# Seven block products for each projection of a pair of heads, in a decoder layer whose first stage is a delta rule

## The chip, the cores and the metric

The kernel runs on one core of a Trainium2 chip. The metric is the device time of one execution in microseconds (us). Before the change the median of three runs is 3437.4 us (3436.95 to 3442.61). A core has five engines that run beside one another, each with a queue of its own: PE multiplies matrices, DVE (VectorE), ACT (ScalarE) and POOL (GpSimd) work on vectors, and SP (SyncE) issues most of the transfers. SBUF is the working memory on the chip, PSUM the memory into which PE writes.

## What is computed

One decoder layer on x of 4 batches x 512 tokens x 512 channels, all in f32: a gated delta rule, then cross-attention with rounded (fake-quantised) values, then self-attention and a mixture of experts. The change touches the first of them alone. Its reference, cut:

```python
q = _causal_conv(x @ Wq.T, cw_q, cb_q)     # conv over 4 tokens per channel, then silu
k = _causal_conv(x @ Wk.T, cw_k, cb_k)
v = _causal_conv(x @ Wv.T, cw_v, cb_v)
...
def step(Sstate, inputs):                  # 16 heads of 128 channels, 512 steps
    retrieved = einsum('bhkv,bhk->bhv', Sstate, k_t)
    error = v_t - g_t[..., None] * retrieved
    Snew = g_t[..., None, None] * Sstate + k_t[..., :, None] * (beta_t[..., None] * error)[..., None, :]
    o_t = einsum('bhkv,bhk->bhv', Snew, q_t)
...
o = o * rsqrt(mean(o * o) + EPS) * norm_w
o = o * silu(x @ Wg.T)
return o @ Wo.T
```

Each of the four weights Wq, Wk, Wv and Wg is 2048 x 512, so that one head's projection of one batch is a product of 128 x 512 by 512 x 512.

## The kernel before

The first stage works through 32 **pairs of heads** (`NP = B * NHG`: 4 batches x 8 pairs of 2 heads). Three stages of work belong to a pair m. `stage1` (L597) makes k and q: projection, conv, transposes, the triangular matrix `at` with its decays, and the products of q with k. `stage2_inverse` (L723) inverts the blocks of `at` in 31 small steps of two operations on POOL (on DVE for pairs 0 and 1), with a way through DRAM at its start and end. `stage2_values` (L768) makes v and the gate g. `stage3` (L813) runs through the four chunks of 128 tokens with a state that each chunk hands to the next, and `output` (L933) multiplies with Wo.

A projection is made in `conv` (L572). For each head it runs four matmuls with 512 columns into one PSUM bank (L578), one for each block of 128 input channels. For q, k and v follow an Identity with scale and bias on ACT (L586), three shifted multiply-adds on DVE that read the projection in PSUM (L589), and a Silu on ACT (L592); for g a Silu alone (L582). The weights of a pair and one projection come in one load of 512 KB (`load_weights`, L564), one buffer for each of the four projections.

**What sets the order.** DVE, ACT and POOL issue their instructions in the order in which the program writes them (`manual_schedule`, L1050). The program is a set of Python generators that yield between steps, and `turns` (L192) takes steps of each in rotation. In the loop of L1066, iteration m takes a step of `stage3(m)` and then one turn of the rest: two steps of `stage1(m + 2)`, one of `stage2_values(m + 1)`, two of the inversions, one of the next batch's `prologue`, where there is one, and one of `output(m - 1)`. `stage3` has some 15 steps; what is left of the others afterwards runs behind it.

Other lines that the steps below name: L642 the scan that makes the decays of a head (one instruction over 4 chunks, with the table `id4`), L666 to L668 `product` (q with k), L685 the multiply of q with its decay on POOL, L698 to L704 the squares of q summed over channels, L731 and L732 the inversion's two operations, L881 `r` and L903 the state in `stage3` on DVE, L888 the matmul that needs `r`, L911 and L928 larger POOL operations of `stage3`, L957 the sums of `output`, L972 the sum with x at a batch's end. `x_kT` and `wpj` (L1074 to L1083) are operands of cross-attention, loaded in the last two iterations, in which the cross-attention of the first tokens already begins.

Of the kernel before, what the change touches and what calls it, by code (L numbers as in the profile page):

```python
# [31 lines left out]
F32 = mybir.dt.float32  # L32
BF16 = mybir.dt.bfloat16
# [29 lines left out]
C_UP, C_LO, C_ONE, C_ID4, C_INV, N_TAB_A = 0, 1, 2, 3, 7, 7 + 8 // GRP  # L63
# [3 lines left out]
def _tables():  # L67
# [10 lines left out]
    ta[:, C_ID4 : C_ID4 + 4] = (r == c)[:, None, :]  # L78
# [26 lines left out]
def decoder(ctx: ExitStack, tc: tile.TileContext, a: dict, out: bass.AP):  # L105
# [21 lines left out]
    def rsqrt(dst, src, pool, add=0.0, mul=1.0):  # L127

        n = src.shape[1]
        t = pool.tile([P, 64], F32, name="rsq")  # L130
        nc.vector.tensor_scalar(t[:, :n], src, mul, add, ALU.mult, ALU.add)  # L131
        nc.gpsimd.tensor_tensor(dst, t[:, :n], mhalf[:, :n], ALU.pow)  # L132
# [233 lines left out]
    with ExitStack() as st:  # L366
# [16 lines left out]
        id4 = tab_a[:, C_ID4 : C_ID4 + 4, :].rearrange("p a b -> p (a b)")  # L383
# [21 lines left out]
        r_d = [dram.tile([HG * TB, P], F32, name=f"r_d{n}") for n in range(SLOTS)]  # L405

# [42 lines left out]
        def prologue(b):  # L449
# [18 lines left out]
            for c in range(TB):  # L468
# [7 lines left out]
                if c == 0:  # L476
                    xnT = s2.tile([P, KD, S], F32, name="xnT", bufs=2)
                    seqs[b] = [xnT]
# [18 lines left out]
            g_a, lg, beta, gam, ngam, gend, gall = (seq.tile([P, H1, TB], F32, name=n) for n in ("g_a", "lg", "beta", "gam", "ngam", "gend", "gall"))  # L497
# [60 lines left out]
            yield  # L558

        sums = {}  # L560

        weights = {}

        def load_weights(m, *what, by=nc.sync):  # L564

            for n in what:
                if m < B * NHG:
                    t = (s1 if n < 2 else s2).tile([P, KD, HG * P], F32, name=f"w{n}", bufs=1)
                    by.dma_start(t, a["a_w"][m % NHG][:, n])
                    weights[m, n] = t  # L570
# [24 lines left out]
        keys, pairs = {}, {}  # L595

        def stage1(m):  # L597
# [3 lines left out]
            wk, wq = weights.pop((m, 1)), weights.pop((m, 0))  # L601

            def rows(n):
                t = s1.tile([P, HG, S], F32, name=f"row{n}", bufs=1)
# [3 lines left out]
            kT, kt = [], []  # L608
            ss = small.tile([P, HG * TB], F32, name="ss", bufs=2)
            for p in range(HG):  # L610
                t = live.tile([P, S], F32, name="kT")
                yield from conv(b, hg, p, 1, wk, t)
                kT.append(t)
                yield
            xnT, beta, gam, ngam, gend, gall = seqs[b]
            gb = rows(0)
            load_weights(m + 1, 1)
# [21 lines left out]
            for p in range(HG):  # L639

                e = s1.tile([P, TB, P], F32, name="em")
                nc.vector.tensor_tensor_scan(chunks(e), gb[p], id4, 0.0, ALU.mult, ALU.add)  # L642
# [17 lines left out]
            qh, qg, pt, sq, kd_ = [], [], [], [], []  # L660

            def product(p):
# [4 lines left out]
                t = live.tile([P, TB, P], F32, name="pt", bufs=6)  # L667
                nc.vector.tensor_tensor(t, pq, em[p], ALU.mult)  # L668
                pt.append(t)

# [5 lines left out]
            for p in range(HG):  # L676
                q = s1.tile([P, S], F32, name="qh")
                c = conv(b, hg, p, 0, wq, q)
                yield from itertools.islice(c, 2)
                if p:  # L680
                    product(0)
                yield from c
                qh.append(q)
                g = live.tile([P, S], F32, name="qg", bufs=6)
                nc.gpsimd.tensor_tensor(g, q, mb[p], ALU.mult)  # L685
                qg.append(g)
                t = w2.tile([P, S], F32, name="cv", bufs=5)
                nc.scalar.activation(t, q, AF.Square)
                sq.append(t)
                yield  # L690
            load_weights(m + 1, 0)
            decayed(0)
            yield
# [11 lines left out]
            yield  # L705
            product(1)
# [3 lines left out]
            keys[m] = (kT, kd_, qg, pt, nr, rq)  # L710
# [57 lines left out]
        def stage2_values(m):  # L768
# [3 lines left out]
            wv, wg = weights.pop((m, 2)), weights.pop((m, 3))  # L772
            v_, gs = [], []
            for p in range(HG):
                t = yield from conv(b, hg, p, 2, wv, None)
                yield
# [963 lines left out]
```

## Time and profile before

| what | value |
|---|---|
| median of the runs | 3437.4 us (3436.95 to 3442.61) |
| the profiled execution's own time | 3435.95 us |
| its span (first to last instruction) | 3434.2 us |
| granted TensorE clock, mean | 0.978 |
| the projections' matmuls (L578) | 2048 records, 592 ns median length, from 19.8 to 1802.2 us |
| the shifted multiply-adds (L589) | 576, mean 746 ns |
| inversion on POOL (L731, L732) | 930 each, mean 344 and 372 ns |
| DMA over the span | 473.97 MB, mean 138 GB/s |

The profile is one execution on the chip. A busy row gives an engine's busy time and its share of the span. The row of 40 slices gives the busy share in tenths. A group row has the line, engine, operation, output and inputs by name, shape and count, then busy time, the mean length of one instruction and the idle time before them with what ended it. [...] The delta rule lies in about the first 1880 us of the span.

### The profile page before, as it was taken

How to read it: one execution, taken by the hardware profiler on the slowest of the kernel's cores; microseconds unless marked ns; L12 is line 12 of the kernel's file. 1: busy time of each engine (PE TensorE's matmuls, PEld its weight loads, DVE VectorE, ACT ScalarE, POOL GpSimd, SP SyncE). 2: the span in 40 equal slices, each digit the busy share in tenths (PEclk: the TensorE clock that was granted, in tenths of full speed). 3: DMA queues.
4: the chain of work that ended last, by engine and by line, in shares of the span. 5: the costliest groups of instructions: out<-in, count | busy, mean ns of one | idle time of the engine just before them, and what ended most of it. 6: DMA issues, size and time to landing. Idle time of an engine off the chain costs nothing. (4 is left out here: it accounts for less than half of the span.)

```text
span 3434.2 us, 49083 instructions
## 1 busy us (share of the span) xinstructions
PE 3253.7 (95%) x16596; PEld 1815.8 (53%) x16596; DVE 1836.7 (53%) x4155; ACT 1600.1 (47%) x4336; POOL 1449.6 (42%) x2766
## 2 busy tenths in 40 slices
PE   5899999999999999999997899999999999999996
PEld 2455555555555555555554455555555545554443
DVE  5755565555645556555545566656655665655111
ACT  3445555455554555455534345455454545534121
POOL 1156766667566675766752211121112111212442
PEclk7999999999999999999998899999999999999998
DMA  6343434534445343453432654445445544546444
GB/s 172 111 124 110 135 110 123 162 110 130 112 122 157 117 134 110 123 151 114 131 103 68 226 181 158 144 159 186 152 142 164 167 153 145 159 165 221 90 83 95
DMA packets 462250, 473.97 MB, mean 138 GB/s; under 512 B 199199, under 2 KB 310821, under 8 KB 461808
## 3 DMA queue, kind: packets, MB, share of 16 engines
q1 hardware_dynamic: 448656, 440.66, 42.2%
q0 software_dynamic: 11904, 27.34, 3.9%
q8 instruction: 132, 2.16, 0.3%
q10 hardware_dynamic: 1440, 2.84, 0.3%
q14 instruction: 118, 0.97, 0.1%
HBM read 410.15 MB, written 64.81 MB: 138 GB/s over the span
## 5 line engine op out<-in xcount | busy, mean ns | idle before, releaser
L578 PE MATMUL pb<-xnT,w 128*128 128x512 f32 x2048 | 959.4, 603 | 0.1
L578 PEld LDWEIGHTS pb<-xnT,w 128*128 128x128 f32 x2048 | 364.3, 192 | 337.4 <-issue 330.9
L589 DVE SCALAR_TENSOR_TENSOR cv<-pb,pp,cv 128x510 f32<-128x510 f32 (+2 forms) x576 | 424.3, 746 | 99.0 <-ACT cv L586 85.7
L732 POOL TENSOR_TENSOR iT<-iT,iW 64x126 f32<-64x126 f32 (+22 forms) x930 | 345.6, 372 | 72.8
L1229 PE MATMUL pb<-c_q,hT 128*128 128x512 f32 x768 | 362.9, 611 | 2.9 <-DMA c_q<-in_c_wk_dram 2.7
L731 POOL TENSOR_TENSOR iW<-iA,iT 64x126 f32<-64x126 f32 (+22 forms) x930 | 320.2, 344 | 65.8 <-issue 0.2
L952 PE MATMUL pb<-wot,og 128*128 128x512 f32 x512 | 246.0, 604 | 6.4 <-DVE xa L957 4.3
L1153 POOL TENSOR_TENSOR rope_s<-q,tab 128x128 f32<-128x128 f32 x64 | 36.6, 572 | 461.2 <-DVE q L1259 403.4
L1229 PEld LDWEIGHTS pb<-c_q,hT 128*128 128x128 f32 x768 | 144.6, 197 | 157.2 <-issue 153.5
L586 ACT ACTIVATE cv<-pb,pp 128x512 f32<-128x512 f32 x192 | 148.7, 774 | 147.5 <-PE pb L578 143.6
L633 POOL TENSOR_TENSOR rk<-ss,mhalf 128x8 f32<-128x8 f32 x32 | 78.0, 2438 | 277.3 <-DVE ss L632 277.3
L957 DVE TENSOR_TENSOR xa<-pb,xa 128x512 f32<-128x512 f32 x112 | 77.1, 689 | 189.8 <-PE pb L952 189.7
L1325 PE MATMUL po<-eT,val 128*128 128x512 f32 x320 | 167.2, 619 | 11.6 <-ACT eT L1323 8.6
L295 ACT ACTIVATE x_e<-pb,nm,x_step 128x256 f32<-128x256 f32 x256 | 141.2, 563 | 75.5 <-DVE nm L291 68.0
L1295 PE MATMUL pb<-kT,qT 128*128 128x256 f32 (+3 forms) x576 | 166.5, 416 | 0.7 <-ACT og L1301 0.6
L1335 PE MATMUL pw<-wot,oT 128*128 128x512 f32 x344 | 163.5, 602 | 0.4 <-DVE oT L1327 0.2
L685 POOL TENSOR_TENSOR qg<-qh,row 128x512 f32<-128x512 f32 x64 | 82.1, 1283 | 176.7 <-ACT qh L592 153.9
L952 PEld LDWEIGHTS pb<-wot,og 128*128 128x128 f32 x512 | 92.2, 191 | 101.8 <-issue 88.9
L1630 PE MATMUL pb<-w_gu,eT 128*128 x312 | 142.1, 599 | 2.0 <-issue 2.0
L1323 ACT COPY eT<-pb 128x512 f32<-128x512 f32 x160 | 90.8, 594 | 107.1 <-PE pb L1321 106.8
L592 ACT ACTIVATE qh<-cv 128x512 f32<-128x512 f32 x64 | 40.3, 630 | 213.0 <-DVE cv L589 205.1
L132 POOL TENSOR_TENSOR rms_r<-rsq,mhalf 128x1 f32<-128x1 f32 x48 | 27.4, 571 | 245.1 <-DVE rsq L131 245.0
(390 smaller groups left out, 6216.6 us busy)
## 6 DMA issues: line engine op xcount, KB each, us to landing
c_q<-in_c_wq_dram SPq DMA_DIRECT2D x128, 512.0 KB
w<-in_a_w_dram SPq DMA_DIRECT2D x124, 512.0 KB
wot<-in_c_wo_dram SPq DMA_DIRECT2D x86, 512.0 KB
row<-g_d SPq DMA_DIRECT2D x64, 512.0 KB
c_o<-in_c_wo_dram SPq DMA_DIRECT2D x42, 512.0 KB
at_d<-at SPq DMA_DIRECT2D x64, 256.0 KB
T<-t_d SPq DMA_DIRECT2D x32, 512.0 KB
X<-x_d SPq DMA_DIRECT2D x32, 512.0 KB
```

The costliest lines, as they stand in the source:

```text
L295: nc.scalar.activation(e[:, 2 * r + g, :], ps[r][:, g, :], AF.Exp, bias=nm[:, r, g : g + 1], scale=step[:, h : h + 1], accum_out=ssum[:, g ...
L578: nc.tensor.matmul(pj, wt[:, kd, p * P : (p + 1) * P], xnT[:, kd, :], start=kd == 0, stop=kd == KD - 1)
L586: nc.scalar.activation(ac, pj, AF.Identity, bias=cb[:, m, h : h + 1], scale=cw[:, m, h, 3:4])
L589: nc.vector.scalar_tensor_tensor(ac[:, j:], pj[:, : S - j], cw[:, m, h, 3 - j : 4 - j], ac[:, j:], ALU.mult, ALU.add)
L731: eng.tensor_tensor(u, A[:, i, i + 1 :].unsqueeze(2).to_broadcast([nb, n, w]), T[:, i, :w].unsqueeze(1).to_broadcast([nb, n, w]), ALU.mult)
L732: eng.tensor_tensor(T[:, i + 1 :, :w], T[:, i + 1 :, :w], u, ALU.add)
L952: nc.tensor.matmul(pw, og[p][:, c * P : (c + 1) * P], wot[:, p, :], start=p == 0, stop=p == HG - 1)
L1229: nc.tensor.matmul(pj, hT[:, kd, :], w[:, kd % 2, :], start=kd == 0, stop=kd == KD - 1)
L1295: nc.tensor.matmul(ps[:, m, k * P : (k + w) * P], qT[g][:, n + m, :], kT[:, g, j : j + w, :], start=True, stop=True)
L1325: nc.tensor.matmul(po, val[:, g, :], eT, start=k == 0, stop=k == c)
L1335: nc.tensor.matmul(pw, oT[:, h + m, :], w[:, m, :], start=g == 0 and h + m == 0, stop=g == 3 and h + m == 3)
L1630: nc.tensor.matmul(pg, hT[:, kd, :], w_gu[:, bass.ds(e, 1), kd, :, :], start=kd == 0, stop=kd == KD - 1)
```

## The change

Two heads' projection is one product of weights (512 inputs x 256 outputs) with the input (512 x 512 tokens). The change cuts each into 2 x 2 blocks: inputs in halves of 256, outputs by head, tokens in halves of 256. Strassen's algorithm, in the form with few additions, makes the four result blocks from seven block products in place of eight; each block product is two matmuls of 256 columns. It needs four sums of weight blocks, four of input blocks, and seven sums that put the products together.

- **Weight sums.** In the first batch, the weights are loaded in two transfers per projection, summed in place (four operations of 128 x 256, `combine`, on POOL or DVE), and the seven blocks are kept in DRAM (`seven_d`). Later batches load all seven blocks in one transfer of 896 KB. All projections share three buffers `w`; a fixed list `order` says which is loaded, summed and stored next.
- **Input sums.** `differences` makes four on POOL, once for each batch.
- **Result sums.** `seven` copies two blocks from PSUM on ACT, adds five on DVE with one operand in PSUM, and adds two in SBUF on POOL. The result lies in SBUF, where Identity, the multiply-adds and Silu then read it, first for both heads.
- **What stays.** k and q of pairs 0 and 1, and v and g of pair 0, run as before (`is_plain`).
- **Room.** Both decay rows share a buffer, as do q and its product with the decay; the scan runs in four pieces with `ident` in place of `id4`; `xnT` has one buffer per parity of batch; `pt` has five buffers instead of six, and `product(1)` and `decayed(1)` wait until `stage3` is done (`busy`); `x_kT` is loaded in the last iteration instead of the one before; `wk` of the cross-attention's keys lies in other tiles.

The diff, cut to its core:

```diff
+        order = [(0, 1), (0, 0), (1, 1), (0, 2), (1, 0), (0, 3)]
+        for m in range(B * NHG):
+            order += [(m + 2, 1), (m + 1, 2), (m + 2, 0), (m + 1, 3)]
...
+        def is_plain(m, n):
+            return m < (2 if n < 2 else 1)
...
+        def differences(b, t1):
+            xnT = seqs[b][0]
+            t = (s2 if b % 2 else s1).tile([P, 3, 2, S // 2], F32, name="xd", bufs=1)
+            b11, b12, b21, b22 = (xnT[:, 2 * k : 2 * k + 2, n * S // 2 : (n + 1) * S // 2] for k in range(2) for n in range(2))
+            for dst, x, y in ((t[:, 1], b22, b12), (t1, b12, b11), (t[:, 0], b22, t1), (t[:, 2], b21, t[:, 0])):
+                nc.gpsimd.tensor_tensor(dst, x, y, ALU.subtract)
+                yield
+            moving[b] = (b11, b21, t1, t[:, 2], t[:, 0], t[:, 1], b22)
...
+        def combine(eng):
+            u = order[stages["combine"]] if stages["combine"] < len(order) else None
+            if u in fresh:
+                a11, a12, s1_, a22, s2_, s3_, s4_ = (fresh[u][:, n] for n in range(7))
+                for dst, x, y, op in ((s3_, a11, s1_, ALU.subtract), (s1_, s1_, a22, ALU.add), (s2_, s1_, a11, ALU.subtract), (s4_, a12, s2_, ALU.subtract)):
+                    eng.tensor_tensor(dst, x, y, op)
...
+        def used(m, n):
+            i = order.index((m, n))
+            keep_them()
+            combine(nc.gpsimd if m < 3 else nc.vector)
+            load()
+
+        def seven(b, n, wt, dst):
+            x = moving[b]
+            def products(*ns):
+                ps = p_b.tile([P, 2, S // 2], F32, name="pb")
+                for k, n in enumerate(ns):
+                    for kd in range(2):
+                        nc.tensor.matmul(ps[:, k], wt[:, n, kd, :], x[n][:, kd, :], start=kd == 0, stop=kd == 1)
+                return ps[:, 0], ps[:, 1]
...
+            l, r = products(0, 4)
+            nc.scalar.copy(c11, l)
+            plus(c12, c11, r)
+            yield
+            l, r = products(5, 2)
+            nc.scalar.copy(c22, r)
+            plus(c21, c12, l)
+            plus(c12, c12, c22, nc.gpsimd)
+            plus(c22, c21, c22, nc.gpsimd)
+            yield
+            l, last_ = products(1, 3)
+            plus(c11, c11, l)
+            yield
+            l, _ = products(6)
+            plus(c21, c21, last_)
+            plus(c12, c12, l)
+            yield
...
+            yield from seven(b, n, wt, dst)
+            used(m, n)
+            for p in range(HG):
+                h = hg * HG + p
+                ac = w2.tile([P, S], F32, name="cv", bufs=5)
+                nc.scalar.activation(ac, dst[p], AF.Identity, bias=cb[:, n, h : h + 1], scale=cw[:, n, h, 3:4])
+                for j in range(1, 4):
+                    nc.vector.scalar_tensor_tensor(ac[:, j:], dst[p][:, : S - j], cw[:, n, h, 3 - j : 4 - j], ac[:, j:], ALU.mult, ALU.add)
+                yield
+                res.append(ac)
+            for p in range(HG):
+                nc.scalar.activation(res[p] if n == 2 else dst[p], res[p], AF.Silu)
+            yield
...
-                nc.vector.tensor_tensor_scan(chunks(e), gb[p], id4, 0.0, ALU.mult, ALU.add)
+                for c in range(TB):
+                    nc.vector.tensor_tensor_scan(e[:, c, :], gb[p][:, c * P : (c + 1) * P], ident, 0.0, ALU.mult, ALU.add)
...
+            yield from convs(m, 0, qh)
+            square(0)
+            square(1)
+            yield
+            product(0)
+            yield
             decayed(0)
...
+            while busy:
+                yield
             product(1)
...
+                x_kT = v_keep.tile([P, 3, KD, M], BF16, name="x_kT")
+                nc.sync.dma_start(x_kT, x_kT_d)
...
+            busy.append(m)
             for _ in stage3(m):
                 next(rest, None)
+            busy.clear()
```

## The prediction

> **What bounds the kernel now.** I read the page's busy rows and slices first, then the engines' busy time inside the delta-rule stage, then groups by form, then the order of time on PE, DVE and POOL.
>
> ```profile
> span 3434.2 us, 49083 instructions
> PE 3253.7 (95%) x16596; PEld 1815.8 (53%) x16596; DVE 1836.7 (53%) x4155; ACT 1600.1 (47%) x4336; POOL 1449.6 (42%) x2766
> ...
> PE   5899999999999999999997899999999999999996
> ...
> POOL 1156766667566675766752211121112111212442
> PEclk7999999999999999999998899999999999999998
> ```
>
> PE is full from slice 2 to slice 20, the stage that the change edits; POOL, 42% over the span, is at 60 to 70% there. The table of engine busy time for 200 to 1700 us (columns: stretch, length, PE, PEld, DVE, ACT, POOL, granted clock, DMA share, GB/s):
>
> ```profile
> 200.00:1700.00 1500.00, 1480.97 (x8709) 862.01 (x8709) 822.63 (x1423) 777.27 (x2195) 1002.68 (x2128) 1.00 0.44 127
> ```
>
> 28 pairs of heads pass in it (rows with one instruction per pair count 28), so a pair takes 1500/28 = 53.6 us: PE 52.9, POOL 35.8, DVE 29.4, ACT 27.8. PE's clock is whole. The stage is bound by PE, and the 24 us that DVE idles per pair are mostly waits for PE:
>
> ```profile
> POOL rk L633 <- DVE ss L632: 216.8, 28, 11.9
> DVE xa L957 <- PE pb L952: 170.4, 69, 3.8
> ACT cv L586 <- PE pb L578: 124.6, 62, 2.9
> ```
>
> **PE: what the seven products take away.** The projection group has 2048 records for 4 x 32 x 2 x 4 = 1024 matmuls of the code, so an f32 matmul counts twice. Busy time is no price, since records overlap; the distance from start to start is. In order of time (start, length):
>
> ```profile
> 1001.44 1.88 PE L578 MATMUL pb<-xnT,w 128*128 128x512 f32 x4
> 1003.16 0.61 PE L888 MATMUL ps<-r,X 128*128 128x128 f32 x4
> ```
>
> Four 512-column records from 1001.44 to 1003.16: 0.430 us each. Half the columns with a new weight block each time is seen in attention:
>
> ```profile
> 2995.72 1.03 PE L1295 MATMUL pb<-kT,qT 128*128 128x256 f32 x4
> 2996.58 0.61 PE L311 MATMUL pb<-ident_i,x_ei 128*128 128x128 bf16 x8
> ```
>
> Four in 0.86 us: 0.215 each, exactly half, so the doubled number of weight loads per column costs nothing visible. A projection of a pair was 8 matmuls, 16 x 0.430 = 6.88 us; it becomes 14 matmuls, 28 x 0.215 = 6.02. It saves 0.86. Of 4 x 32 = 128 projections 6 stay plain (k and q of pairs 0 and 1, v and g of pair 0): **122 x 0.86 = 105 us off PE**, 3.44 per pair. PE's floor falls from 53.6 (its present gaps kept) to 50.1 us per pair.
>
> **What comes on the other engines.** Prices from groups by form:
>
> ```profile
> L589 DVE SCALAR_TENSOR_TENSOR cv<-pb,pp,cv 128x510 f32<-128x510 f32 x168 | 125.8, 749 | 5.9
> ...
> L685 POOL TENSOR_TENSOR qg<-qh,row 128x512 f32<-128x512 f32 x56 | 71.4, 1275 | 115.0 <-ACT qh L592 93.7 <-issue 21.4
> ...
> L642 DVE TENSOR_TENSOR_SCAN em<-row,tab_a 128x512 f32<-128x512 f32 x56 | 65.3, 1208 | 0.0
> ```
>
> and, for 128x256 with one operand in PSUM, from the later stages:
>
> ```profile
> L1633 DVE TENSOR_TENSOR xa<-xa,pb 128x256 f32<-128x256 f32 x39 | 16.4, 421 | 184.1 <-ACT xa L1632 184.1
> ```
>
> - DVE: five 128x256 adds with one PSUM operand per projection, 5 x 0.42 x 4 = 8.4 us per pair. The scan in four pieces: nothing if time goes with columns; at most three extra fixed costs of 0.2 (a scalar_tensor_tensor of 128 columns takes 0.34, of 512 0.745, so 0.2 is there without columns), 1.2 per pair for two scans. I take 0.9. DVE: 29.4 + 9.3 = 38.7.
> - ACT: two 128x256 copies per projection at 0.37 (L700, same size from PSUM): 2.9 per pair; 30.7. Silu of g from SBUF is 0.63 against 0.60: nothing.
> - POOL: two 128x256 adds per projection. 64x136 takes 0.47, 128x512 1.275; between them some 0.75. 8 x 0.75 = 6.0; 41.8 per pair. The q multiply is only moved.
> - Weight sums: 32 sets of four 128x256 operations. Eight fall to POOL (8 x 4 x 0.75 = 24 us, in the prologue and the first two iterations, where POOL was 10 to 25% busy until 200 us), 24 to DVE in iterations 1 to 7: 24 x 4 x 0.42 = 40 us, about 6 per pair. There DVE is at 45 of 50. Each waits for its load, issued one projection earlier; behind a late one DVE's or POOL's whole queue waits.
> - Input differences: four 128x512 POOL operations per batch, 5 us, once per batch: in the numbers above, nothing. Bounds 0 to 5 us for the first, which runs ahead of iteration 0.
> - DMA: 6 x 0.5 + 32 x 0.5 MB, 32 stores and 90 loads of 0.92 MB instead of 128 x 0.52: 64 MB more over 1.7 ms, 38 GB/s beside 127 at 44% share. Three buffers, loaded three projections (some 38 us) ahead: cost 0; if that cover went, SP's queue (T, X, rrow loads behind it) would stop on a buffer. Bounds 0 to 10 us.
> - x_kT is loaded one iteration later, with wpj. The wpj load was issued at 1802.8 and the first matmul on x_kT ran at 1804.6. 0.77 MB will not have landed: 3 us lost, bounds 0 to 8.
> - Buffers: both decay rows share one, so the second row's load waits for the scans and holds SP's queue until then; its reader, the POOL multiply, comes some four turns later: 0, bounds 0 to 1 us per pair. The second head's product and its scaling on ACT move behind stage3: PE work of 0.9 us per pair that no longer fills gaps inside stage3 but fills the end of the iteration: 0, bounds -0.5 to 0.9 per pair. The smaller tables and rsq tiles cost nothing, since no instruction goes with them.
>
> **The coupling.** Two things decide how much of 105 us arrives. First, the convolution's three scalar_tensor_tensors read PSUM and SBUF today; after, both tensors lie in SBUF, as do those of L972. What that does beside POOL is in the trace:
>
> ```profile
> 1052.05 0.74 DVE L972 SCALAR_TENSOR_TENSOR xa<-xa,a_rs,x_in 128x512 f32<-128x512 f32 x1
> ...
> 1056.18 1.16 DVE L972 SCALAR_TENSOR_TENSOR xa<-xa,a_rs,x_in 128x512 f32<-128x512 f32 x1
> ```
>
> ```profile
> 1055.52 1.27 POOL L911 TENSOR_TENSOR gs<-gs,rrow 128x512 f32<-128x512 f32 x1
> 1056.75 0.76 POOL L731 TENSOR_TENSOR iW<-iA,iT 64x81 f32<-64x81 f32 x1
> ```
>
> The first L972 runs between POOL's work in 0.74; the second starts inside L911 and takes 1.16, and POOL's next takes 0.76 where its group's mean is 0.37. So each delays the other by about 0.4 when they meet. There will be 18 such DVE operations per pair; if each catches one POOL instruction, POOL gets 18 x 0.39 = 7 us and stands at 48.8, DVE some 18 x 0.2 = 3.6 (between nothing and 0.42) and stands at 42. Both are still under 50.1, POOL just so.
>
> The Trainium skill ("SBUF — State Buffer", Who interferes with whom) says that a VectorE instruction with two SBUF inputs and a GpSimd instruction that reads SBUF exclude each other for the whole instruction. By that rule POOL's 41.8, 18 x 0.745 and two scans of 1.2 could not overlap at all: 57.6 us per pair, an estimate, some 120 us slower in 30 pairs. The rows above agree that they exclude each other, but only in part: the second L972 ended 0.2 us sooner than a start after L911 would allow.
>
> Second, hand-overs. A conv went PE, ACT, DVE, ACT; now it goes PE, ACT, DVE, POOL, DVE, ACT, DVE, ACT, and each wait holds an in-order queue: behind DVE's wait for POOL's sums stand r and state of stage3, for which PE waits. Chain after the last product: 2 x 0.42 + 0.775 + 3 x 0.745 + 0.63 = 4.5 us for the first head, 6.7 for the second, against 3.6 before. Cover in the order of emission: two to three turns of about 3.4 us before a transpose or product uses it. So mostly hidden, with little left when POOL is a turn late. Per pair the loss lies between 0 and 3.4 us (all the gain) or beyond; I take a third of the gain, 1.2, because POOL has 1.3 of 50.1 us free for waits where it has 18 today.
>
> **Sum**, against the profiled execution's own 3435.95 us (span 3434.2 and 1.75 around it): -105 + 31 x 1.2 (37) + first batch, DVE near full, 6 x 2 = 12 + x_kT 3 = -53: 3383. The median of the runs lies 1.45 above that execution: **3385**.
>
> **Rivals.**
> - Nearly all of it arrives (waits under 0.5 us per pair): 3340 to 3360. For it: DVE's idle time is mostly waiting for PE. Chance 0.15.
> - **Slower: POOL becomes the bound.** Place: the inversion's small operations among the convs of two heads. It passes PE when POOL gets 8.3 us of delays per pair, and passes today's 53.6 at 11.8, which is 30 of its 84 instructions held 0.39 us; 18 DVE operations catching two each give 36, 14 us: 55.8 per pair, 2.2 x 30 = 66 and 15 for the first batch and x_kT on top: up to 3515; where POOL's waits add only 1 us per pair to 53.6, 3470. For it: POOL's long wait for ss cannot be filled, since its queue is in order. Against: the count of one catch each. Chance 0.36.
> - Nothing: gain and waits cancel, 3430 to 3444. Chance 0.08.
> - That 256 columns do not run at half: excluded by L1295.
>
> **How the numbers follow.** Forecast case 3360 to 3430: 0.41. Faster 0.41 + 0.15 = 0.56; within 0.2% (7 us, about what a measurement of this kernel can tell from no change) 0.08; slower 0.36. Range 3340 to 3470: it leaves out some 0.05 below and 0.14 above. The forecast case's own range is 3360 to 3430.
>
> **What would show it.** Right: PE's projection records 3416 of 256 columns at 0.215 start to start, pair time 51 to 52 us, POOL 80 to 95% in the stage. POOL's inversion groups 10 to 20% longer than today, conv operations above 0.8. Wrong: PE idle before L888 or its conv consumers with DVE as releaser, and DVE waiting on POOL's sums: then POOL or the chain is the bound. Wrong the other way: PE still 98% busy and the pair at 50.

## The result and the profile after

The kernel after takes 3661.0 us (median of 4 runs, 3659.5 to 3662.7) against 3437.2 of the kernel before on the same chip: ratio 1.0653, 95% interval 1.0631 to 1.0675. It is 224 us slower where 52 us less was forecast, far outside the range. The page of the kernel after, busy rows and slices:

```profile
span 3660.7 us, 53930 instructions
...
PE 3252.2 (89%) x18060; PEld 2139.6 (58%) x18060; DVE 2163.0 (59%) x5053; ACT 1681.6 (46%) x4580; POOL 1851.2 (51%) x3059
...
PE   5778878899889888898888789999999999999997
...
POOL 1368777888778888688888221112111211211442
PEclk7889999999999999999999889999999999999998
```

PE is no longer full in the slices of the delta-rule stage, which now ends in slice 23; no other engine is full in its place. Nearly everything happens inside the delta-rule stage: from the first `og` of pair 0 to that of pair 31 it takes 1889.7 us against 1682.4 (+207), the work ahead of it 14 more, the work behind it 5 more.

Below, an **ordinary pair** is one without a batch's edge or a prologue beside it (the mean of eight, from one pair's first `og` to the next one's): 52.8 us before, 56.4 after. Over 31 pairs these 3.6 us make 112 of the 207 us; the others lie in the first batch and in the four pairs around each later prologue, which take 62 to 69 us in the second batch against 53 to 60 before. The engines' busy time over two ordinary pairs, before and then after (stretch, length, PE, PEld, DVE, ACT, POOL, clock, DMA share, GB/s):

```profile
681.43:787.01 105.58, 105.07 (x619) 60.90 (x618) 55.20 (x91) 53.78 (x154) 71.31 (x153) 1.00 0.43 123
```

```profile
784.50:897.30 112.80, 101.51 (x715) 79.27 (x714) 72.72 (x143) 58.75 (x171) 94.79 (x169) 1.00 0.48 145
```

PE stands still for 0.25 us per ordinary pair before and for 5.7 after (my sum of the gaps between one matmul record's end and the next one's start; the ends are modelled by the profiler, so this serves to compare).

The whole stage, from the first `og` of pair 0 to that of pair 31, before and then after:

```profile
195.62:1877.98 1682.36, 1640.53 (x9760) 956.86 (x9758) 912.80 (x1603) 858.37 (x2421) 1086.14 (x2287) 0.99 0.43 123
```

```profile
209.42:2099.12 1889.70, 1634.30 (x11182) 1263.75 (x11180) 1225.81 (x2463) 938.73 (x2661) 1465.55 (x2553) 0.96 0.47 142
```

PE idles for 255 us of it instead of 42, and its granted clock is lower, 0.96 instead of 0.99. What PE waits for, over the whole run of after (total, times, longest):

```profile
PE pb L803 <- ACT qg L704: 60.1, 27, 4.8
PE ps L1009 <- DVE r L1002: 30.6, 33, 6.6
PE pb L1073 <- DVE xa L1078: 19.8, 22, 2.2
...
PE ps L1019 <- ACT u L1011: 15.9, 19, 1.0
```

No single wait is the loss: the Silu of q, `r`, `u` and banks that DVE has not yet read come one after the other. DVE's, ACT's and POOL's largest waits in after that answer to those shown of before:

```profile
ACT qg L704 <- DVE cv L700: 148.4, 57, 4.8
POOL rk L763 <- DVE ss L762: 146.4, 32, 22.4
...
ACT cv L698 <- DVE qg L644: 92.8, 30, 6.2
DVE kT L644 <- POOL kT L644: 78.5, 23, 5.0
...
DVE xa L1078 <- PE pb L1073: 47.4, 38, 3.5
```

The same of before, over its whole run too:

```profile
ACT qh L592 <- DVE cv L589: 205.1, 59, 11.5
DVE xa L957 <- PE pb L952: 189.7, 80, 4.8
...
ACT cv L586 <- PE pb L578: 143.6, 70, 3.8
```

Before, DVE waited 190 us for PE at this sum of `output`; now 47 us are left. ACT waited 144 us for PE at the convs' Identity, and now waits 93 us there for DVE's sums. That ACT waits for DVE at the Silu of q is not new: 205 us before, 148 after.

### The profile page after: what moved, and what is told of

Same layout as the page of the kernel before. It is cut to its first block, busy times and chain, and to the rows that moved or that the text cites. A ratio compares the mean times of both kernels' runs of the same rounds, so it can differ in the third digit from the quotient of the medians.

```text
span 3660.7 us, 53930 instructions
## 1 busy us (share of the span) xinstructions
PE 3252.2 (89%) x18060; PEld 2139.6 (58%) x18060; DVE 2163.0 (59%) x5053; ACT 1681.6 (46%) x4580; POOL 1851.2 (51%) x3059
## 5 line engine op out<-in xcount | busy, mean ns | idle before, releaser
L640 PE MATMUL pb<-xnT,w 128*128 128x256 f32 x1952 | 533.6, 400 | 33.4 <-DVE at L785 14.1
L861 POOL TENSOR_TENSOR iT<-iT,iW 64x126 f32<-64x126 f32 (+22 forms) x930 | 418.5, 450 | 72.9
L860 POOL TENSOR_TENSOR iW<-iA,iT 64x126 f32<-64x126 f32 (+22 forms) x930 | 418.8, 450 | 67.9 <-DMA iA<-at_d 4.1
L640 PE MATMUL pb<-xd,w 128*128 128x256 f32 x1464 | 391.5, 396 | 27.6 <-POOL xd L574 16.5
L640 PEld LDWEIGHTS pb<-xd,w 128*128 128x128 f32 x1464 | 285.4, 199 | 79.9 <-DVE xa L1078 20.0
L644 DVE TENSOR_TENSOR kT<-kT,pb 128x256 f32<-128x256 f32 x150 | 60.5, 420 | 273.1 <-ACT kT L649 122.2
L700 DVE SCALAR_TENSOR_TENSOR cv<-kT,pp,cv 128x511 f32<-128x511 f32 x180 | 148.8, 839 | 32.9 <-ACT cv L698 28.6
L700 DVE SCALAR_TENSOR_TENSOR cv<-qg,pp,cv 128x511 f32<-128x511 f32 x180 | 148.6, 825 | 25.4 <-ACT cv L698 21.2
L803 PE MATMUL pb<-qg,kT 128*128 128x128 f32 x512 | 92.9, 305 | 60.1 <-ACT qg L704 60.1
L700 DVE SCALAR_TENSOR_TENSOR cv<-vn,pp,cv 128x511 f32<-128x511 f32 x186 | 139.1, 748 | 4.4
```

The source lines that it names most:

```text
L640: nc.tensor.matmul(ps[:, k], wt[:, n, kd, :], x[n][:, kd, :], start=kd == 0, stop=kd == 1)
L700: nc.vector.scalar_tensor_tensor(ac[:, j:], dst[p][:, : S - j], cw[:, n, h, 3 - j : 4 - j], ac[:, j:], ALU.mult, ALU.add)
L803: nc.tensor.matmul(pq[:, c, :], kT[p][:, cs], qh[p][:, cs], start=True, stop=True)
L860: eng.tensor_tensor(u, A[:, i, i + 1 :].unsqueeze(2).to_broadcast([nb, n, w]), T[:, i, :w].unsqueeze(1).to_broadcast([nb, n, w]), ALU.mult)
L861: eng.tensor_tensor(T[:, i + 1 :, :w], T[:, i + 1 :, :w], u, ALU.add)
```

## The experiments

All ratios are to the kernel before on the same chip, with 95% intervals. "Pair" is the ordinary pair, before 52.8, after 56.4.

Three theories went in. **A**: POOL's added sums, and the SBUF access that DVE and POOL share, make DVE late and with it PE. **B**: the longer way of a conv behind the last product, with both heads together, in queues that run in order. **C**, a rival to both, was the re-arrangement itself (buffers, scan, order). In B, B1 is the distance to a conv's own consumer, and B2 the hops of `stage3` that stand behind a conv.

### Is it the products or the re-arrangement?

```diff
-            return m < (2 if n < 2 else 1)
+            return True                       # e1: no projection with seven products
+            return n < 3 or m < 1             # e3: g alone
+            return n < 2 or m < 1             # e13: v and g
```

In these three the plain projections read an input block that the differences have replaced (in batch 0 from the end of its first pair on), so their values are not the layer's; all instructions are there.

> The kernel after, with every projection made as before (eight block products, conv from PSUM); what is left of the change is its re-arrangement: three shared weight buffers, one buffer for both decay rows, the scan in four pieces, q and its decayed product in one buffer, product(1) behind stage3, x_kT an iteration later, and the input differences on POOL. Theory A (POOL's added sums and the shared SBUF access of DVE and POOL delay DVE and so PE) and theory B (the longer chain of hand-overs and the burst of six multiply-adds) put no cost here: 3437 + 3 for x_kT + at most 10 = 3435 to 3450 us. Theory C (the re-arrangement itself makes the waits) expects a large part of the 224 us here: 3500 us or more.

> The kernel after, with seven products for g alone; k, q and v as before, their multiply-adds reading PSUM. PE saves 31 x 0.86 = 27 us; POOL gets 1.5 us per pair, DVE 2.1 and no SBUF-only multiply-add; g has no conv behind it. Theory A and theory B: nearly all of it arrives, less some 3 us each for x_kT and for a quarter of the weight sums: 3410 to 3430 us. Theory C: above 3480 us.

> The kernel after, with seven products for v and g, k and q as before. From g alone (3459 us) to all four (3661 us) stand 201 us for k, q and v. If each of them costs the same (their DVE and POOL work is alike): 3526 us. Theory B1 (the consumer of q, product(0), and those of k, the transposes, come soonest; v's transposes have a turn more): v costs little, 3460 to 3490 us. Theory B2 (v's six multiply-adds come in two turns, three at a time, as stage2_values takes one step a turn): the same, 3460 to 3490 us.

Measured: e1 3443.4 us (1.0022, 1.0007 to 1.0038), pair 52.1, as A and B expected: C falls. e3 3459.5 us (1.0076, 1.0055 to 1.0096), outside both ranges: g alone, which has no conv, saves nothing. Per ordinary pair projections take PE 27.17 us instead of 27.99 (0.82 of the 0.86 forecast), but the other matmuls take 0.9 more, half of it in gaps, and the pair stays at 52.1. e13 3720.8 us (1.0834, 1.0814 to 1.0853), pair 61.1: **worse than all four together**, against every expectation. PE waits 136 us at v's transposes (L906) for v's Silu, a wait that after hardly has, and the granted clock is 0.94 in its ordinary pairs, where it is 1.00 in those of after. So the cost does not add up projection by projection.

### POOL

e2 gives DVE the two sums that POOL makes; e5 leaves out 30 of the 31 inversion steps; e4 is the kernel before with another operand:

```diff
-            plus(c12, c12, c22, nc.gpsimd)    # e2
-            plus(c22, c21, c22, nc.gpsimd)
+            plus(c12, c12, c22)
+            plus(c22, c21, c22)
...
+                if i:                          # e5, in stage2_inverse
+                    yield i
+                    continue
...
-                nc.vector.scalar_tensor_tensor(ac[:, j:], pj[:, : S - j], ...      # e4, L589 of before
+                nc.vector.scalar_tensor_tensor(ac[:, j:], xnT[:, 0, : S - j], ...
```

> The kernel after, with the two sums of each projection that POOL makes given to DVE. POOL loses 8 x 0.75 = 6 us per pair, DVE gets 8 x 0.42 = 3.4, and the hand-over DVE, POOL, DVE is gone. Theory A (DVE stands behind late sums of POOL): the pair goes from 56.4 to 53 or 54 us, the whole to 3560 to 3610 us. Theory B (DVE's own burst of both heads' multiply-adds holds r and the state): DVE gets longer, 3650 to 3700 us. Theory C: no change, 3661 us within 10.

> The kernel after, with 30 of the 31 steps of each pair's inversion left out (60 of its 62 multiply-add operations, on POOL for all but the first two pairs); the order and the number of turns stay. POOL is then nearly empty and hardly any of its work meets DVE's. Theory A (POOL's load and the shared SBUF access make DVE, and with it PE, late): an ordinary pair goes from 56.4 to 51 to 53 us, the whole to 3500 to 3560 us. Theory B (the consumers stand too near behind a longer chain in queues that run in order): 54.5 to 56 us per pair, 3600 to 3650.

> The kernel before, in which the three multiply-adds of each conv read the input x in SBUF in place of the projection in PSUM, so the conv's shifted terms are left out and replaced. Same instructions, same order, same waits: only the memory of one operand changes, 18 operations per pair. Exclusion as I priced it: POOL's inversion groups go from 344 and 372 ns to 430 to 460, POOL from 35.8 to about 42 us per pair, the conv operations from 0.75 to 0.80 to 0.95. Theory A expects that POOL has the room here, 0 to 1.5 us per pair: 3437 to 3485 us. If the exclusion alone were the cause of the loss, without POOL's sums and the longer chain: 3550 us or more. Theories B and C: 3437 us within 7.

Measured: e2 3668.0 us (1.0682, 1.0661 to 1.0703), pair 57.3, in the ranges of B and C. e5 3584.1 us (1.0440, 1.0413 to 1.0466); POOL's busy time falls from 47.4 to 21.7 us per pair, and the ordinary pair only from 56.4 to 55.6. The time lies between the two ranges, the pair in B's. Most of the 77 us that come back are in the work ahead of the first pair (19), the first batch (22) and the pairs beside prologues. **Theory A falls as the main cause**: neither POOL's sums nor its load holds the ordinary pair.

e4 3475.8 us (1.0123, 1.0103 to 1.0144), pair 54.2. It prices the shared access alone. Its groups:

```profile
L589 DVE SCALAR_TENSOR_TENSOR cv<-xnT,pp,cv 128x510 f32<-128x510 f32 (+2 forms) x576 | 515.3, 903 | 99.4 <-ACT cv L586 85.7
...
L732 POOL TENSOR_TENSOR iT<-iT,iW 64x126 f32<-64x126 f32 (+22 forms) x930 | 400.7, 431 | 72.9
L731 POOL TENSOR_TENSOR iW<-iA,iT 64x126 f32<-64x126 f32 (+22 forms) x930 | 376.1, 404 | 65.7 <-issue 0.2
```

The conv operations go from 746 to 903 ns, the inversion's from 344 and 372 to 404 and 431. Over the run DVE gets 89 us more and POOL 128, so 0.15 and 0.22 us for each of 576 operations. It is the meeting with POOL that costs: the 139 of the 576 that ran beside no POOL instruction took 0.746 us, the other 437 took 0.953, while before the 367 that ran beside one took 0.746 as well (my count). POOL has plenty of room, at 40 of 54 us, and still 39 us are lost: 2.8 us more DVE per pair cost 1.4 us of time. This was the first sign that a conv's time counts although DVE is half idle.

### The convs on DVE and their order

e10 leaves out two of the three shifted multiply-adds; e6 moves `product(0)`; e9 spreads the multiply-adds; e14 moves the Silus:

```diff
+                    if j == 1:                 # e10: only this one is made
                         nc.vector.scalar_tensor_tensor(ac[:, j:], dst[p][:, : S - j], ...
+                    if j == 2 and n < 2:       # e9
+                        yield
...
-            product(0)                         # e6
             yield
             decayed(0)
...
+            product(0)
             while busy:
...
+            for _ in range(2 if n < 2 else 1): # e14, ahead of the Silus in convs
+                yield
```

> The kernel after, with two of the three shifted multiply-adds of each conv left out: 12 operations, 9 to 10 us of DVE, per pair. If PE waits for what stands on DVE in the convs (theories B1 and B2), the ordinary pair goes from 56.4 to 52 or 53 us, the whole to 3530 to 3570 us, more than the 77 us that came with an empty POOL. If the loss lies in the hand-overs of the products' sums (PE, ACT, DVE, POOL, DVE) ahead of the conv, 55 us per pair and 3610 us or more.

> The kernel after, with product(0), q with k of the first head, emitted two turns later, ahead of the wait for the end of stage3; the number of turns stays. PE waits at this product for the Silu of q in 27 of 32 pairs, 60 us in all. Theory B (too little cover in the order of emission): most of the 60 us goes, 3600 to 3630 us. Theory A (the engines behind are short of time, whichever consumer shows it): the wait comes up at another place, 3645 to 3665 us.

> The kernel after, with the three multiply-adds of each head of k and q handed out over two turns' steps (a yield after the second), so that DVE runs at most three of them in a turn before it comes to r and the state of stage3, in place of six (5.25 us in one stretch in the trace). Theory B2 (stage3's hops, r on DVE, u on ACT, the state on DVE, stand in order behind the burst and behind the Silus that wait for its end): 1 to 2 us per pair less, 3600 to 3635 us. Theory B1 (it is the distance from a conv to its own consumer that is short): the conv ends later, product(0) follows later as well, 3650 to 3670 us.

> The kernel after, with the two Silus of each conv one turn later (two more yields for k and q, one for v), so that ACT meets u of stage3 before it stands for DVE's second head of multiply-adds. Theory B2 (ACT's in-order queue stands at the Silu and holds u, DVE's burst holds r and the state): 1 to 2 us per pair less, 3600 to 3630 us. Theory B1 (the consumer comes too soon behind the conv, and everything that ends the conv later makes it worse): product(0) and the transposes move back with the Silus, or wait longer; 3660 to 3720 us.

Measured: e10 3491.8 us (1.0177, 1.0159 to 1.0195), pair 51.7: 169 us come back, the most of all edits that keep the seven products of all four projections and more than the range expected, and 4.7 us per pair for 9.3 us of DVE. So the multiply-adds weigh far more than POOL's load (e5); whether by DVE's time or by the length of the chain that they stand in, e10 does not say. But no move of an emission helped:

- e6 3690.1 us (1.0748, 1.0722 to 1.0774), pair 57.9, slower than either theory had it. The wait at `product(0)` is gone; 94.4 us at L1019 for `u` came instead.
- e9 3670.9 us (1.0698, 1.0678 to 1.0718), pair 57.3. 99.7 us at v's transposes came instead.
- e14 3659.1 us (1.0654, 1.0637 to 1.0672), pair 58.2. Of the wait for q's Silu 7.0 us are left, and of `u` 10.7 us. Instead PE waits 48.7 us for the inverse to come back from DRAM and 35.4 us for `r`.

How a conv holds the state's chain can be read in e6, in order of time (start, length, engine and line, wait):

```profile
844.66 0.75 PE L1009 MATMUL ps<-r,X 128*128 128x128 f32 x4 [0.24 <-DVE r L1002]
844.78 2.85 DVE L700 SCALAR_TENSOR_TENSOR cv<-qg,pp,cv 128x511 f32<-128x511 f32 x3
...
847.72 0.63 ACT L704 ACTIVATE qg<-cv 128x512 f32<-128x512 f32 x1 [3.26 <-DVE cv L700]
...
848.26 0.35 ACT L649 COPY cv<-pb 128x256 f32<-128x256 f32 x1
848.51 0.44 ACT L1011 COPY u<-ps 128x128 f32<-128x128 f32 x2
...
848.83 0.86 PE L1019 MATMUL ps<-u,kdec 128*128 128x128 f32 x4 [3.43 <-ACT u L1011]
```

PE has finished X times r at 845.4. `u` is a 0.44 us copy on ACT, but ACT stands 3.26 us at the Silu for DVE's multiply-adds of q, and `u` is queued behind it: PE stands 3.43 us. This shows that mechanism in e6. That it is the whole loss in after was theory B2. e14 speaks against its half on ACT: with the Silus behind `u` the time was the same. e9 speaks against its half on DVE, for k and q. No run moves both at once.

### The order of the heads and the way over SBUF, without seven products

e12 is the re-arrangement alone: e1 without the input differences (their calls for batch 0 are out too). The next three add to e12, with eight products and no sums: e15 both heads' matmuls first, a copy of each projection to SBUF by ACT, then both convs as in after; e18 the copy alone, for q, k and v, head by head as before; e19 the order without the copy, the conv reading PSUM.

```diff
-            if b:                              # e12, with is_plain as in e1
-                yield from differences(b, xnT[:, 0:2, S // 2 :])
...
+            for p in range(HG):                # e15, in place of seven; e19 without the copy
+                pj = p_b.tile([P, S], F32, name="pb")
+                for kd in range(KD):
+                    nc.tensor.matmul(pj, wt[:, kd, p * P : (p + 1) * P], seqs[b][0][:, kd, :], ...)
+                    if kd == 1:
+                        yield
+                nc.scalar.copy(dst[p], pj)
+                yield
...
+            nc.scalar.copy(held, pj)           # e18, in conv; Identity and L725 then read held
```

> The kernel with the re-arrangement alone: all projections in eight block products and without the input differences, which nothing reads then. The whole layer is computed. With the differences it took 3443 us, an ordinary pair 52.07 us against 52.79 before, but the pairs beside a prologue 61.3 and 55 to 56.6 against 59.5 and 52.8. If the differences (four operations of 128x512 on POOL, each at the end of a turn) cost these 3 to 4 us three times: 3430 us; if they also cost the 11 us of the first batch: 3420 us. If they cost nothing, as I predicted: 3443 us.

> The re-arrangement alone (an ordinary pair 52.05 us, 3425 us in all), and added to it only the order of the two heads: eight products as before, each head's projection copied to SBUF by ACT, then, behind both heads, Identity, multiply-adds and Silus as in the kernel after, from SBUF. No seven products, no sums on DVE or POOL, no weight sums, no input differences. Known beside it: the multiply-adds from SBUF cost 1.4 us per pair by themselves. If the order of the two heads and the burst of six multiply-adds make the waits (theory B): 55 to 58 us per pair, 3510 to 3600 us. If the sums of the block products make them: 53 to 54 us per pair, 3450 to 3490 us.

> The other half of the run with both heads in the new order (58.2 us per ordinary pair, 3593 us): here the projections of q, k and v are copied to SBUF by ACT and the conv reads them there, as in that run, but head by head, in the order of before. If the order of the two heads makes the waits: 52.05 us, 1.4 for the multiply-adds from SBUF and up to 1 for the copies: 53.4 to 54.5 us per pair, 3465 to 3500 us. If the way over SBUF with one hand-over more makes them: 56 to 58 us per pair, 3550 to 3600 us.

> Both heads in the new order with eight products, but the conv, and the Silu of g, read the projections in PSUM: no copy, no multiply-add with two operands in SBUF. Both banks of a conv are held until its last multiply-add, which before held one at a time. If the order of the two heads makes the waits: 55 to 57.5 us per pair, 3510 to 3580 us (the upper end where the held banks add to it). If the copies and the access to SBUF make them: 52 to 53.5 us per pair, 3425 to 3470 us.

| kernel | conv | us | ratio and interval | pair |
|---|---|---|---|---|
| e12 | head by head, from PSUM | 3425.1 | 0.9976 (0.9967 to 0.9985) | 52.1 |
| e18 | head by head, from SBUF | 3533.3 | 1.0296 (1.0278 to 1.0314) | 56.8 |
| e19 | both heads, from PSUM | 3623.4 | 1.0582 (1.0536 to 1.0627) | 58.0 |
| e15 | both heads, from SBUF | 3593.3 | 1.0457 (1.0440 to 1.0474) | 58.2 |

The engines' busy time over two ordinary pairs of e12 and of e15, columns as above:

```profile
675.60:779.68 104.08, 103.57 (x619) 61.55 (x618) 55.03 (x102) 53.30 (x154) 69.39 (x152) 1.00 0.46 123
```

```profile
730.33:846.72 116.39, 107.83 (x619) 62.76 (x618) 56.70 (x103) 61.80 (x170) 78.53 (x153) 0.99 0.42 114
```

The same 619 matmul records, 0.8 us more DVE per pair, 4.3 more ACT and 4.6 more POOL, all three engines under 40 of 58 us, and the pair is 6.1 us longer. The waits of PE in e15, and then in e18:

```profile
PE ps L1029 <- ACT u L1021: 56.8, 30, 2.6
PE ps L1019 <- DVE r L1012: 44.3, 34, 3.5
```

```profile
PE pb L947 <- DMA T<-t_d: 75.1, 23, 5.6
PE pb L750 <- ACT kT L727: 25.2, 31, 4.0
```

In e15 it is `u` and `r`, so `stage3`; in e18 the inverse from DRAM and the Silu of k. PE's largest waits in e19:

```profile
PE pb L792 <- DVE cv L710: 51.2, 26, 2.0
PE pb L640 <- ACT Y L984: 25.3, 30, 0.9
PE pb L981 <- DVE xa L1088: 19.6, 25, 0.8
```

In all three PE waits for an engine whose result it does not read: a multiply-add, a copy and a sum that still read a bank of `pb`, which has four. So what e19 shows is in the main the banks held twice as long, and the order by itself stays unmeasured. **The way over SBUF is enough by itself for a loss**: 4.7 us per pair and 108 us in all (e18), against 6.1 us and 168 for the whole new way of a conv (e15). My expectation that only the order counts was wrong: e18's pair is in the rival's range, its time below it, and e19 is slower than both its ranges. The granted clock blurs these pairs: it is 0.97 over two of e18's, 0.99 over two of e15's and 1.00 in e12 and after, which can stand for up to 1.3 us of e18's pair and 1.1 of e15's (half of the time per pair in which the trace's clock is at 0.5).

### The sums, and the single parts

```diff
-            plus(c12, c12, c22, nc.gpsimd)     # e17: these four left out
-            plus(c22, c21, c22, nc.gpsimd)
-            plus(c11, c11, l)
-            plus(c21, c21, last_)
...
-                    eng.tensor_tensor(dst, x, y, op)   # e7: no weight sums, three loads instead
+                    pass
...
             while busy:                        # e8: this in the kernel before, ahead of product(1)
                 yield
...
-                if p:                          # e16: in the kernel before, behind both heads instead
-                    product(0)
```

> The kernel after, with four of the seven sums of each projection left out: both of POOL's and two of DVE's five (the ones that wait for a block of the second and third pair of products); 3.4 us less DVE and 6 us less POOL per pair, and no hand-over DVE, POOL, DVE. The multiply-adds stay. If the sums make the waits: 53 to 54 us per pair, 3550 to 3590 us. If the multiply-adds of both heads behind the last product make them (theory B): 55 to 56 us per pair, 3610 to 3650 us.

> The kernel after, with the four operations of each weight sum left out and the three blocks that they make loaded in their place, so 32 sets of four operations of 128x256 are missing and 12 MB more are loaded. The prediction put them at 12 us in the first batch: 3649 us if that holds. The first batch takes 458 us in after against 388 with all projections plain, 18 more than the second batch loses, and the work ahead of it 18 more: if all of that is the sums, 3625 us. Nothing to do with theories A and B in the other batches.

> The kernel before, with one part of the re-arrangement: the second head's product of q with k and its scaling wait until stage3 is done. With all projections plain and the whole re-arrangement an ordinary pair takes 52.07 us against 52.79. If this move is the reason: 31 x 0.7 = 22 us less, 3412 to 3420 us. If the 0.7 comes from another part of the re-arrangement: 3437 us within 7.

> The kernel before, with product(0) made behind both heads of q, in place of between the second head's first two steps and its conv. It is the other difference in order between before and the re-arrangement, whose ordinary pair takes 0.74 us less. If this move is the reason: 3415 to 3425 us; if not (then the shared row buffer, the scan in pieces or the squares behind both heads): 3437 us within 7.

Measured: e17 3637.3 us (1.0587, 1.0569 to 1.0605), pair 56.8, its time in B's range: the sums are not what holds the pair. e7 3629.4 us (1.0573, 1.0549 to 1.0597): the weight sums cost some 30 us, 26 of them in the first batch's stage and 8 ahead of it by the two traces. Their groups in after:

```profile
L614 DVE TENSOR_TENSOR w<-w 128x256 f32<-128x256 f32 x96 | 49.9, 520 | 2.5
...
L614 POOL TENSOR_TENSOR w<-w 128x256 f32<-128x256 f32 x32 | 24.3, 759 | 6.0 <-DMA w<-in_a_w_dram 4.1
```

e8 3434.1 us (0.9999, 0.9988 to 1.0010): `product(1)` behind `stage3` costs and gains nothing. e16 3427.1 us (0.9979, 0.9968 to 0.9991): one moved call, with one yield more, makes the kernel before 7 us faster, so that it and e12 **beat both kernels**. Of e12's 0.74 us per pair this move gives 0.34; where the rest is from stays open.

## Why the prediction was wrong, point by point

- **PE's saving: right.** Five groups of four 256-column records of a projection in after, in order of time:

```profile
1872.23 1.13 PE L640 MATMUL pb<-xnT,w 128*128 128x256 f32 x4
1873.19 1.03 PE L640 MATMUL pb<-xd,w 128*128 128x256 f32 x4
1874.06 1.03 PE L640 MATMUL pb<-xnT,w 128*128 128x256 f32 x4
1874.92 1.03 PE L640 MATMUL pb<-xd,w 128*128 128x256 f32 x4
1875.78 1.03 PE L640 MATMUL pb<-xnT,w 128*128 128x256 f32 x4
1876.65 1.88 PE L1073 MATMUL pb<-wot,og 128*128 128x512 f32 x4
```

  0.87 us from group to group, 0.217 a record; 3416 such records. The 105 us are off PE's work at full clock. They hardly show in PE's busy time of the stage (1640.5 before, 1634.3 after): some 57 us went to the lower clock (next point), and some 40 are not accounted for. Nor do they become time, because PE idles 213 us more.
- **"PE's clock is whole" was carried over to after, and is wrong there.** In order of time, with the clock of the second stretch below:

```profile
1205.71 1.13 PE L640 MATMUL pb<-xnT,w 128*128 128x256 f32 x4
1206.67 1.03 PE L640 MATMUL pb<-xd,w 128*128 128x256 f32 x4
1210.03 1.22 PE L1000 MATMUL ps<-state,kT 128*128 128x128 f32 x4 [2.32 <-DVE state L1024]
1211.04 1.91 PE L640 MATMUL pb<-xnT,w 128*128 128x256 f32 x4
1212.75 0.93 PE L1009 MATMUL ps<-r,X 128*128 128x128 f32 x4
```

```profile
1210.00:1213.40 3.40, 3.38 (x12) 3.02 (x13) 2.00 (x7) 0.00 (x0) 3.10 (x7) 0.50 1.02 343
```

  Behind a wait of 2.3 us the clock is 0.50, and four records take 1.71 us to the next start in place of 0.87 to 0.96. In the stage the trace has 28 such stretches of half clock in after, 154 us in all, against 5 and 34 us before. Each of the 28 begins behind 6.8 us in which PE idled for at least 1.6 us in sum; not every such idle time has one behind it. Where the distance between two matmuls of a stream is about doubled, the excess adds up to 79 us in after and 21 before (my count). So some 57 us of the loss, an estimate, are PE at half clock behind its own waits.
- **Prices of the added operations: right or near.** Groups of after (busy time, mean ns of one):

```profile
L773 DVE TENSOR_TENSOR_SCAN em<-row,tab 128x128 f32<-128x128 f32 x256 | 100.1, 452 | 5.9 <-DMA row<-g_d 5.9
...
L644 DVE TENSOR_TENSOR kT<-kT,pb 128x256 f32<-128x256 f32 x150 | 60.5, 420 | 273.1 <-ACT kT L649 122.2 <-POOL kT L644 78.5 <-PE pb L640 56.9
...
L644 POOL TENSOR_TENSOR kT<-kT 128x256 f32<-128x256 f32 x60 | 43.5, 725 | 14.8 <-DVE kT L644 12.5
```

  The DVE adds take 0.41 to 0.42 us (0.42 forecast), POOL's 0.73 to 0.81 (0.75), the scans 8 x 0.45 against 2 x 1.21, so 1.2 more per pair (0.9, bound 1.2). DVE stands at 36.4 us per ordinary pair (42), POOL at 47.4 (48.8), ACT at 29.4 (30.7).
- **The shared access.** I had 0.2 us for DVE and 0.39 for POOL at each operation; e4 measures 0.15 and 0.22. In after itself the inversion's operations take 450 ns each, 31 and 21% more than before (10 to 20% forecast), and the multiply-adds 0.80 us (above 0.8 forecast). By the Trainium skill ("SBUF — State Buffer", Who interferes with whom) the two exclude each other for the whole instruction. e4 disagrees: per ordinary pair its multiply-adds and POOL's work together cover 43.8 us, where the lengths that they have in before, one behind the other, would need 48.9. Wrong was the next step, "both are still under 50.1", taken for no cost: there is one of 1.4 us per pair with POOL at three quarters.
- **The failed step: "Cover in the order of emission: two to three turns of about 3.4 us before a transpose or product uses it. So mostly hidden", with 1.2 us per pair.** The lengths of the chain were stated; the cover was counted to the conv's own consumer only, and taken for free time. Forecast were 51 to 52 us for a mean pair of 53.6, so some 50.5 for an ordinary one of 52.8; it takes 56.4. With all of the gain it would take 49.4, so the term of 1.2 us measures 7.0. e15 has the new way of a conv with none of the products, sums or differences, and is 165 us slower than e12 (1.0457 - 0.9976, times 3433). e18 has one copy and the SBUF operands and is 110 slower. So the delay of a conv was not covered. How it comes through is shown at one place (the trace of e6) and otherwise argued: `stage3`, the inversion's way through DRAM and the three convs share in-order queues, and what ends later in one place ends the next chain later.
- **First batch: the term of 12 us is some 30.** The 96 operations of the 24 sums on DVE take 0.52 us each instead of 0.42, which is 10 us of the difference; the rest stays open.
- **Input differences at 0 (bounds 0 to 5): some 16** (e1 against e12, 1.0022 - 0.9976). In e12 the pair behind a prologue returns to 52.0 us; in e1 it takes 54.9 to 56.6.
- **product(1) at 0: right** (e8). x_kT's 3 us: the work behind the stage takes 1561.5 us against 1556.2, but 1556.4 in e14, which loads it just as late; not to be told apart.
- **The slower rival: right in sign, wrong in mechanism.** POOL was to become the bound. It is busy 47 of 56 us, and emptied it gives back 0.8 us per pair.

**Where the 224 us come from**, as far as the runs can be added up (e13 says that such sums are rough; each term has its share of the lower clock): re-arrangement -8, input differences 16, the conv's new way 165, weight sums 27 to 32; 21 are left for all sums of the products less whatever of PE's 105 us arrives. Four of the seven sums account for 23 (e17). In the ordinary pair seven products with their sums are even 1.8 us faster than eight in the same order (56.4 against 58.2, of which up to 1.1 are e15's lower clock), so some of the gain may be there, on top of a way that loses more.

What stays open: which chain is the last in after, and what the order of the heads costs without longer held banks. Every move met another one, and no order of emission was found in which seven products beat the kernel before. With two of three multiply-adds left out after is still slower than before.

## What to carry to other kernels

A full PE row says that the schedule fits, not that the other engines have slack: in this kernel a copy and a slower operand on engines that are half idle cost 4.7 us per pair. The likely reason, seen in single places only, is that other chains, the recurrent one above all, stand in the same in-order queues. Before a bulk saving on the full engine is priced, price the delay: replace only the way of the result (one more copy, another order, the same arithmetic), as e15 and e18 do; it takes few lines and would have foretold a loss here. Look at the granted clock of each stretch as well, before two pair times are compared: waits of PE were followed by half clock here. And when a wait that you remove comes back elsewhere at the same total, shorten the chain itself: three moves gave nothing here, and the multiply-adds that e10 leaves out gave back 169 us.

## What the runs showed of the hardware

- Half the columns take half the time for f32 matmuls, with a new weight block for each (0.430 and 0.217 us a record), also in a projection.
- A multiply-add of 128 x 510 with both tensors in SBUF takes 0.90 us beside a busy POOL against 0.75 with one in PSUM, and each costs POOL 0.22 us (e4); beside no POOL instruction it takes 0.75 there too. The loss is a part of the instruction, not the whole of it (43.8 us covered per pair against 48.9).
- An add of 128 x 256 on DVE takes 0.42 us with one operand in PSUM and 0.52 with both in SBUF, in the same run (L644, L614). All 96 of the latter ran beside a POOL instruction, the shortest in 0.40; of the former, the 526 beside one took no longer than the 84 others (0.416 and 0.418).
- In after's delta-rule stage PE's clock falls to 0.50 in 28 stretches, each behind 6.8 us with at least 1.6 us of PE's idle time; in the one shown above four f32 records of 256 columns take 1.71 us in place of 0.87.
